# A router product with its operands exchanged, in four column groups of the TensorE array, and its accumulation over the tokens in two halves

## The chip, the cores and the metric

The kernel runs on one core of a Trainium2 chip. The metric is the device time of one execution in microseconds (us). Before the change it was 2703.0 us, the median of three runs: 2703.13, 2699.41 and 2703.0.

A core has five engines, each with its own instruction queue. TensorE (PE in the profile; PEld is its loading of stationary operands, the "weights") multiplies matrices into PSUM. VectorE (DVE), ScalarE (ACT) and GpSimd (POOL) work on tiles of 128 partitions in SBUF and PSUM. SyncE (SP) issues most DMA transfers. A semaphore orders the engines wherever one needs what another has made.

## What is computed

The weight of a first layer is corrected by a low-rank product, quantized to a codebook of 32 levels, and corrected again. Its output goes through a second layer and, beside it, through a mixture of eight small experts of rank 16; the input is added at the end. Cut to what matters:

```python
lora_delta = lora_B @ lora_A * (LORA_ALPHA / LORA_RANK)          # 32 / 64
cb = codebook / jnp.clip(jnp.max(jnp.abs(codebook)), 1e-08)
wg = (weight + lora_delta).reshape(O, I // GROUP, GROUP)         # groups of 128
normalized = wg / jnp.exp(scale_log)
idx = jnp.searchsorted((cb[:-1] + cb[1:]) * 0.5, normalized, side='left')
w_eff = (cb[idx] * scale).reshape(O, I) + lora_delta             # in value
x1 = x @ w_eff.T                                                 # first layer

result = x1 @ W_base.T + b_base
ax = x1 @ A_w.T                                                  # rank 16
probs = softmax(x1 @ router_w.T)                                 # 8 experts
per_expert = einsum('bsr,erq->bseq', ax, cores)
mixed = einsum('bseq,bse->bsq', per_expert, probs)
result = result + mixed @ B_w.T * SCALING                        # 32 / 16
return x + result
```

There are 4096 tokens of 2048 features, and both layers have 2048 outputs; all is float32. `A_w` and `router_w` stand one below the other as 24 rows (16 of rank, 8 of experts); the kernel gets them transposed, as `raT`.

## The kernel before

No value of the first layer is computed for a token. The kernel makes the product of both layers' weights, Wc = W_base · w_eff + identity (the identity carries the added input), and the product of the 24 rows with w_eff, and multiplies the tokens by these.

**Stage a** makes the weights, in 16 strips of 128 input features (`NS` = 16; `strip[i]` gives their order). A strip `a` is a tile of 128 partitions by 16 chunks of 128 (`NM` = 16). The order of the instructions is written out by hand: `quantize(i, at)` (L537) goes through the 28 levels from 3 to 30 of strip i, and after each level issues what `behind(r, f, ...)` (L719) has hung behind round r = level - 3. So the rounds of strip i carry the making ready of strip i+1 and the products of strip i-1. Every engine executes its queue in the order in which this program issues.

- `raise_to` (L527) is a round: ScalarE writes a mask into one of two buffers of `mpool` (L532), and VectorE puts the level's value where the mask is set (L533).
- For strip i+1 ScalarE also scales the low-rank correction (L496, rounds 7 and 11) and makes the lowest levels (`level_0`: L509, L512, L514, at rounds 10, 12, 14 and, for the second half, 16, 18, 20); GpSimd does `normalize`, `more_levels` and, at a strip's end, `straight_through` (L552 to L554; on VectorE for the last strip).
- `products(i-1, bs, c)` (L703) multiplies a quarter (4 chunks) of the strip by two of the four output blocks b of W_base: blocks 2 and 0 behind rounds 2, 5, 8 and 11, blocks 3 and 1 behind 17, 20, 22, the last quarter at the start of the next strip. `wb` (blocks 0 and 1) stays in SBUF, `wbp` (2 and 3) is streamed by SP in pieces (L485). A correction `low_rank` (L589) ends each pair.
- `multiply_router(i-1)` (L609), behind round 13, is the product with the 24 rows: 16 matmuls with a chunk of `a` as weights (128 columns) and 24 streamed columns (L612), plus a low-rank one (L615). `keep_router` (L623, round 22) copies the 128x24 result to `rac`, whose 32 columns (`RP` = 32) were cleared by a memset (L256).
- `keep(i, b)` (L618) empties a block's PSUM tile on ScalarE (L620) and stores it in `wc_dram` (L621): blocks 2 and 0 behind rounds 17 and 19, 3 and 1 behind rounds 5 and 6 of the next strip.
- All products of a strip share `psum_m`, three PSUM tiles that are used in turn: m_2, m_0, m_r (the router), m_3, m_1. So m_3 waits until keep has emptied m_2, m_1 waits for m_0's, and the next strip's m_0 waits for m_3's.
- `load_route(i-1)` (L627, round 9) loads the strip's 128 features of all 4096 tokens in four tiles `xs`, and `route` (L634), at the start of the second strip after it, multiplies them by `rac`: eight matmuls of 512 tokens, four to each of two PSUM tiles `acc`, in four groups of 32 array columns (`tile_position`). The sums run over all 16 strips.
- GpSimd makes from `wc_dram` the sums that stage b needs, and SP stores them in `s_dram` (`outer_w`, `inner_some`, `put`, L311 to L349).

After the last strip (L796 to L818) its products follow without other rounds between them. Here ScalarE's queue issues the stores of `wc_dram`, and `late_columns` (L677) makes the last sums on VectorE, from two fetches into tiles named late and last, stored by GpSimd's queue.

**Stage b** (from L821) multiplies the tokens by Wc in the fast scheme with seven products in place of eight, applied twice: 49 products a group of tokens (`product`, L902), each of one 1 MB tile `s` (L856) and a tile of tokens or of differences of tokens (`xA`, `xB`, `xC`, loaded at L850; differences `t` at L880). Its pools take the SBUF that stage a's pools leave, so a tile of stage b can be written only when the tiles of stage a on the same addresses are done with.

The router's product and its place, as the program has it:

```python
for m in range(NM):
    nc.tensor.matmul(ps[:, :NRA], strips[i]["a"][:, m, :], ra_sb[:, m, :], start=(m == 0), stop=False)
nc.tensor.matmul(ps[:, :NRA], strips[i]["la"][:R], lora_r, start=False, stop=True)
...
behind(13, multiply_router, i - 1)
behind(17, keep, i - 1, 2)
```

The first operand after the output is the stationary one (the weights), the second is streamed.

Of the kernel before, what the change touches and what calls it, by code (L numbers as in the profile page):

```python
# [20 lines left out]
P = 128  # L21
# [161 lines left out]
def adaln_ffn_kernel(  # L183
# [72 lines left out]
    nc.gpsimd.memset(rac, 0.0)  # L256
    cb = const.tile([P, K], F32, name="cb")
    ident = const.tile([P, P], F32, name="ident")
    ones = const.tile([P, 1], F32, name="ones")

# [7 lines left out]
    def constants():  # L268
# [3 lines left out]
        nc.gpsimd.tensor_copy(ones, ident[:, Q : Q + 1])  # L272
        for j in range(1, 4):
            nc.gpsimd.tensor_tensor(ones, ones, ident[:, RP * j + Q : RP * j + Q + 1], ALU.add)
# [87 lines left out]
    with ExitStack() as sa:  # L362
# [4 lines left out]
        xsp = sa.enter_context(tc.tile_pool(name="xsp", bufs=4))  # L367
# [106 lines left out]
        ra_sb = cl.tile([P, NM, NRA], F32, name="ra_sb")  # L474
        nc.sync.dma_start(ra_sb, raT)
# [82 lines left out]
        lora_r = cl.tile([R, NRA], F32, name="lora_r")  # L558
# [19 lines left out]
        def lora_router():  # L578
            ps = psum_m.tile([P, OQ], F32, tag="m", name="lc_r")
            for m in range(NM):  # L580
                nc.tensor.matmul(
                    ps[:R, :NRA], lora_B_sb[:, m, :], ra_sb[:, m, :], start=(m == 0), stop=(m == NM - 1)
                )
            nc.scalar.mul(lora_r, ps[:R, :NRA], LORA_SCALE)
# [24 lines left out]
        def multiply_router(i):  # L609
            ps = psum_m.tile([P, OQ], F32, tag="m", name=f"m_{i}_r")  # L610
            for m in range(NM):
                nc.tensor.matmul(  # L612
                    ps[:, :NRA], strips[i]["a"][:, m, :], ra_sb[:, m, :], start=(m == 0), stop=False
                )
            nc.tensor.matmul(ps[:, :NRA], strips[i]["la"][:R], lora_r, start=False, stop=True)  # L615
            strips[i]["r"] = ps

# [5 lines left out]
        def keep_router(i):  # L623
            nc.scalar.copy(rac[:, strip[i], 0:NRA], strips[i]["r"][:, :NRA])


        def load_route(i):  # L627
            strips[i]["x"] = []
            for n in range(4):
                x = xsp.tile([P, 2 * HT], F32, tag="xs", name=f"xs_{i}_{n}")  # L630
                nc.sync.dma_start(x, xT[ts(strip[i], P), ts(n, 2 * HT)])
                strips[i]["x"].append(x)

        def route(i):  # L634
            for n in range(8):
                j = n % 4
                nc.tensor.matmul(
                    acc[n // 4][RP * j : RP * j + RP],
                    rac[:, strip[i], :],
                    strips[i]["x"][n // 2][:, ts(n % 2, HT)],  # L640
# [587 lines left out]
```

## Time and profile before

| what | value |
|---|---|
| median of three runs | 2703.0 us (2699.41 to 2703.13) |
| the profiled execution | 2701.32 us |
| its span | 2699.5 us |
| mean granted TensorE clock | 0.971 of full speed |
| PE busy | 2562.5 us (95%) |
| DVE busy | 1574.9 us (58%) |
| ACT busy | 1117.8 us (41%) |
| POOL busy | 1300.1 us (48%) |
| HBM traffic over the span | 215 GB/s |

The span is what lies between the first and the last instruction in the trace; the execution's own time has a little around it. The shares are means over two unlike stages, as the page's slices show: each digit is the busy share of one of 40 equal slices (67.5 us each), in tenths.

```profile
PE   4699999999999999999799999999999999999999
DVE  9999999999999999973423213233123322224321
ACT  6888988999998888840000000000000000000000
```

The first 17 or 18 slices are stage a, where VectorE and TensorE are both full and ScalarE nearly so; the rest is stage b, TensorE's products alone. The chain that ended last, by engine and by line:

```profile
PE 59%; DVE 22%; ACT 8%; DMA 5%; issue 3%; SPq 2%; POOL 1%; DVEq 0%; POOLq 0%; ACTq 0%
PE z L902 49%; DVE a L533 21%; PE m L601 8%; ACT above L532 6%; PE z L932 1%; DMA wbp<-in_wbT 1%; DMA s<-s_dram 1%; DMA xA<-in_xT 1%; ACT out L620 1%; DMA s_dram<-late_z 1%; ACT a L514 1%; SPq L347 1%; SPq L348 0%; DMA s_dram<-z 0%; ACT sg L509 0%
```

How to read a group: line, engine, operation, output and inputs with their shapes, count | busy us, mean ns of one | idle time of the engine just before them, with what ended most of it. A float32 matmul of the program is two matmul records in the trace (two passes). A row of the timeline has start, length (us), engine, line, what it does, count, and in brackets the idle time before it and its releaser.

### The profile page before, as it was taken

The numbers are of one execution on the slowest core, as the hardware profiler recorded it, in microseconds if no ns is written. First come the engines' busy times: TensorE is split into PE (matmuls) and PEld (weight loads), VectorE is DVE, ScalarE is ACT, GpSimd is POOL, SyncE is SP. The second block draws the span as 40 slices with busy tenths as digits, with TensorE's granted clock in tenths as the row PEclk, the third lists the DMA queues.
The fourth block names the chain that finished last, engine by engine and source line by source line (L and its number), as shares of the span: only waits on it lengthen the run. The fifth ranks groups of instructions, "written<-read, shape, count | busy, mean of one in ns | idle before, by whom it ended". The sixth has DMA issues, their size and how long they took to land.

```text
span 2699.5 us, 26233 instructions
## 1 busy us (share of the span) xinstructions
PE 2562.5 (95%) x10544; PEld 1761.5 (65%) x10544; DVE 1574.9 (58%) x995; ACT 1117.8 (41%) x740; POOL 1300.1 (48%) x751
## 2 busy tenths in 40 slices
PE   4699999999999999999799999999999999999999
PEld 2244444444444444445688888888888888888887
DVE  9999999999999999973423213233123322224321
ACT  6888988999998888840000000000000000000000
POOL 5666668889888888744304232033310313302324
PEclk9799999999999999999899999999999999999999
DMA  7345457766776767699744666545675455854554
GB/s 283 138 167 178 178 174 246 233 229 225 244 242 232 244 219 237 209 314 324 300 174 143 231 245 217 208 142 209 213 264 186 171 206 181 292 194 171 186 198 163
DMA packets 222809, 581.06 MB, mean 215 GB/s; under 512 B 18328, under 2 KB 120608, under 8 KB 177760
## 3 DMA queue, kind: packets, MB, share of 16 engines
q1 hardware_dynamic: 216448, 559.01, 60.2%
q0 software_dynamic: 4640, 13.90, 1.4%
q10 hardware_dynamic: 1600, 6.49, 0.6%
q8 instruction: 83, 1.36, 0.2%
q14 instruction: 38, 0.31, 0.0%
HBM read 477.62 MB, written 101.71 MB: 215 GB/s over the span
## 4 chain that ended last, share of the span: by engine, by line
PE 59%; DVE 22%; ACT 8%; DMA 5%; issue 3%; SPq 2%; POOL 1%; DVEq 0%; POOLq 0%; ACTq 0%
PE z L902 49%; DVE a L533 21%; PE m L601 8%; ACT above L532 6%; PE z L932 1%; DMA wbp<-in_wbT 1%; DMA s<-s_dram 1%; DMA xA<-in_xT 1%; ACT out L620 1%; DMA s_dram<-late_z 1%; ACT a L514 1%; SPq L347 1%; SPq L348 0%; DMA s_dram<-z 0%; ACT sg L509 0%
## 5 line engine op out<-in xcount | busy, mean ns | idle before, releaser
L533 DVE COPY_PREDICATED a<-above,step 128x2048 f32<-128x2048 uint16 (+1 forms) x453 | 1116.5, 2468 | 51.1 <-ACT above L532 5.7
L532 ACT ACTIVATE above<-w,neg_t 128x2048 bf16<-128x2048 f32 (+1 forms) x453 | 899.4, 1991 | 141.7 <-DVE a L533 128.8
L902 PE MATMUL z<-t,s 128*128 128x256 f32 x3584 | 793.5, 381 | 7.1 <-DMA s<-s_dram 7.1
L902 PEld LDWEIGHTS z<-t,s 128*128 128x128 f32 x3584 | 679.1, 190 | 110.9 <-issue 20.0
L601 PE MATMUL m<-wbp,a 128*128 128x512 f32 x1024 | 506.7, 641 | 43.0 <-POOL a L554 35.7
L601 PE MATMUL m<-wb,a 128*128 128x512 f32 x1024 | 467.0, 599 | 26.6 <-ACT out L620 26.6
L601 PEld LDWEIGHTS m<-wbp,a 128*128 128x128 f32 x1024 | 205.7, 206 | 294.4 <-issue 243.9
L601 PEld LDWEIGHTS m<-wb,a 128*128 128x128 f32 x1024 | 194.7, 192 | 276.6 <-issue 238.7
L982 ACT COPY m<-z 128x1024 f32<-128x1024 f32 x28 | 28.4, 1013 | 766.0 <-PE z L902 766.0
L902 PE MATMUL z<-xA,s 128*128 128x256 f32 x1152 | 256.2, 381 | 12.4 <-DMA s<-s_dram 12.4
L993 POOL TENSOR_TENSOR c<-u,m 128x1024 f32<-128x1024 f32 x16 | 50.1, 3129 | 444.1 <-DVE u L990 422.8
L902 PEld LDWEIGHTS z<-xA,s 128*128 128x128 f32 x1152 | 219.8, 191 | 43.7 <-issue 13.6
L521 POOL TENSOR_SCALAR lv<-w,base 128x1024 f32<-128x1024 f32 x60 | 226.9, 3782 | 3.7
L993 POOL TENSOR_TENSOR M<-u,m 128x1024 f32<-128x1024 f32 x8 | 25.7, 3208 | 354.1 <-DVE u L990 296.4
L902 PE MATMUL z<-xB,s 128*128 128x256 f32 x768 | 169.7, 379 | 0.0
L902 PE MATMUL z<-xC,s 128*128 128x256 f32 x768 | 169.7, 379 | 0.0
L984 DVE TENSOR_TENSOR u<-z,m 128x1024 f32<-128x1024 f32 x28 | 34.3, 1223 | 219.0 <-issue 175.5
L902 PEld LDWEIGHTS z<-xB,s 128*128 128x128 f32 x768 | 145.9, 190 | 19.8
L902 PEld LDWEIGHTS z<-xC,s 128*128 128x128 f32 x768 | 145.9, 190 | 19.8
L988 ACT COPY m<-z 128x1024 f32<-128x1024 f32 x28 | 28.3, 1011 | 308.5 <-PE z L902 308.5
L522 POOL TENSOR_TENSOR a<-a,lv 128x1024 f32<-128x1024 f32 x60 | 142.5, 2375 | 18.4 <-ACT a L514 13.8
L552 POOL TENSOR_TENSOR a<-a,w 128x1024 f32<-128x1024 f32 x30 | 71.3, 2376 | 144.3 <-DVE a L533 144.3
(206 smaller groups left out, 1916.6 us busy)
## 6 DMA issues: line engine op xcount, KB each, us to landing
s<-s_dram SPq DMA_DIRECT2D x196, 1024.0 KB, 4.9
wbp<-in_wbT SPq DMA_DIRECT2D x131, 1024.0 KB, 5.2
xs<-in_xT SPq DMA_DIRECT2D x64, 512.0 KB, 7.2
xA<-in_xT SPq DMA_DIRECT2D x24, 1024.0 KB, 9.9
s_dram<-z SPq DMA_DIRECT2D x84, 256.0 KB, 5.6
xB<-in_xT SPq DMA_DIRECT2D x16, 1024.0 KB, 10.6
outT<-M SPq DMA_DIRECT2D x16, 1024.0 KB, 12.7
w<-in_weight SPq DMA_DIRECT2D x15, 1024.0 KB, 7.3
```

The costliest lines, as they stand in the source:

```text
L347: q.dma_start(to[:, n, 1:3, g, c], y[:, n, 1])
L521: v.tensor_scalar(lv, half(i, f, "w"), base[:, c + 1 : c + 2], base[:, c : c + 1], ALU.is_gt, ALU.mult)
L522: v.tensor_tensor(a, a, lv, ALU.add)
L532: nc.scalar.activation(above[:, c], q, AF.Relu, bias=neg_t[:, r : r + 1])
L533: nc.vector.copy_predicated(a, above[:, c].bitcast(U16), step[:, r : r + 1].to_broadcast([P, F // n]))
L552: v.tensor_tensor(a, a, w, ALU.subtract)
L601: nc.tensor.matmul(ps, strips[i]["a"][:, CM * c + m, :], t[:, m, :], start=c == 0 and m == 0, stop=False)
L902: nc.tensor.matmul(z[:, c, :], s[:, k, ts(c, P)], rhs[:, k, :], start=not more and k == 0 and c % PER == 0, stop=k == NK - 1 and c % PER = ...
L982: nc.scalar.copy(temp("m1", o), z["a"])
L984: nc.vector.tensor_tensor(temp("u2", o), z["b"], state["m1", o], ALU.add)
L988: nc.scalar.copy(temp("m5", o), z["c"])
L993: lambda d: nc.gpsimd.tensor_tensor(d, state["u3", o], state["m5", o], ALU.add),
```

## The change

- `ra_sb` has 32 columns in place of 24, the last eight cleared by a memset on VectorE, so its load goes into pieces of 24 of 32 columns. `lora_r` has 32 columns too.
- `multiply_router` exchanges the operands: a chunk of `ra_sb` (32 columns) is stationary and a chunk of the strip (128 columns) streams. Chunk m goes to the group m mod 4 of 32 array columns, and so to 32 partitions of the PSUM tile of its own; the low-rank matmul adds to the first group. The result is 24 of 32 rows by 128 features, in four partial sums.
- `router_parts` (new), behind round 16 and so between the second L509 and the next mask on ScalarE, copies the four partial sums (128x128) to SBUF, as `raw`.
- `router_sum` (new), behind round 17 after the first quarter of blocks 3 and 1, multiplies `raw` as weights by `stack`, four 32x32 unit matrices one below the other, which turns the result back and adds the four parts. `stack` is made in `constants()` by GpSimd.
- `keep_router` copies all 32 columns of `rac`, so its memset goes.
- `load_route` and `route` work on a half of the tokens at a time: `xs` has two buffers in place of four. The first half is loaded behind round 9 as before and multiplied at the start of the second strip after it; the second half is loaded there and multiplied behind round 8, between the second and third quarter of blocks 2 and 0. After the last strip its second half takes the mask buffers of `mpool`.
- After the last strip the parts follow in the order that the diff shows.

```diff
--- before.py
+++ after.py
@@ -253,11 +253,12 @@
     dram = ctx.enter_context(tc.tile_pool(name="dram", bufs=1, space=DRAM))
 
     rac = const.tile([P, NS, RP], F32, name="rac")
-    nc.gpsimd.memset(rac, 0.0)
     cb = const.tile([P, K], F32, name="cb")
     ident = const.tile([P, P], F32, name="ident")
     ones = const.tile([P, 1], F32, name="ones")
 
+    stack = const.tile([P, RP], F32, name="stack")
+
 
     accs = [const.tile([P, HT], F32, name=f"accs_{h}") for h in range(2)]
 
@@ -270,7 +271,9 @@
         nc.gpsimd.memset(cores_sb, 0.0)
 
         nc.gpsimd.tensor_copy(ones, ident[:, Q : Q + 1])
+        nc.gpsimd.tensor_copy(stack, ident[:, 0:RP])
         for j in range(1, 4):
+            nc.gpsimd.tensor_tensor(stack, stack, ident[:, RP * j : RP * j + RP], ALU.add)
             nc.gpsimd.tensor_tensor(ones, ones, ident[:, RP * j + Q : RP * j + Q + 1], ALU.add)
         for j in range(4):
             nc.sync.dma_start(cores_sb[:, j, 0:Q], cores)
@@ -364,7 +367,7 @@
 
         lap = sa.enter_context(tc.tile_pool(name="lap", bufs=4))
         cl = sa.enter_context(tc.tile_pool(name="cl", bufs=1))
-        xsp = sa.enter_context(tc.tile_pool(name="xsp", bufs=4))
+        xsp = sa.enter_context(tc.tile_pool(name="xsp", bufs=2))
         spool = sa.enter_context(tc.tile_pool(name="spool", bufs=2))
         wcp = sa.enter_context(tc.tile_pool(name="wcp", bufs=3))
         big1 = sa.enter_context(tc.tile_pool(name="big1", bufs=1))
@@ -471,8 +474,10 @@
                 m = ts(h, NM // 2)
                 nc.sync.dma_start(t[:, m, :], wbT[b][:, m, :])
             wb.append(t)
-        ra_sb = cl.tile([P, NM, NRA], F32, name="ra_sb")
-        nc.sync.dma_start(ra_sb, raT)
+        ra_sb = cl.tile([P, NM, RP], F32, name="ra_sb")
+        nc.vector.memset(ra_sb, 0.0)
+        nc.sync.dma_start(ra_sb[:, :, 0:NRA], raT)
+        raw = cl.tile([P, P], F32, name="raw")
         NC = 4
         CM = NM // NC
         stream = [(b, c) for b in range(NST, NB) for c in range(NC)] * (NS + 1)
@@ -555,7 +560,7 @@
 
 
         lora_c = cl.tile([2 * R, NB // 2, OQ], F32, name="lora_c")
-        lora_r = cl.tile([R, NRA], F32, name="lora_r")
+        lora_r = cl.tile([R, RP], F32, name="lora_r")
 
         def lora_columns(pair):
             ps = psum_m.tile([P, OQ], F32, tag="m", name=f"lc_{pair}")
@@ -579,9 +584,9 @@
             ps = psum_m.tile([P, OQ], F32, tag="m", name="lc_r")
             for m in range(NM):
                 nc.tensor.matmul(
-                    ps[:R, :NRA], lora_B_sb[:, m, :], ra_sb[:, m, :], start=(m == 0), stop=(m == NM - 1)
+                    ps[:R, :RP], lora_B_sb[:, m, :], ra_sb[:, m, :], start=(m == 0), stop=(m == NM - 1)
                 )
-            nc.scalar.mul(lora_r, ps[:R, :NRA], LORA_SCALE)
+            nc.scalar.mul(lora_r, ps[:R, :RP], LORA_SCALE)
 
         def low_rank(i, bs):
             for b in bs:
@@ -607,13 +612,27 @@
                 load_piece(nc.scalar if i == NS - 1 else nc.sync)
 
         def multiply_router(i):
+
             ps = psum_m.tile([P, OQ], F32, tag="m", name=f"m_{i}_r")
             for m in range(NM):
+                j = m % 4
                 nc.tensor.matmul(
-                    ps[:, :NRA], strips[i]["a"][:, m, :], ra_sb[:, m, :], start=(m == 0), stop=False
+                    ps[RP * j : RP * j + RP, 0:P], ra_sb[:, m, :], strips[i]["a"][:, m, :],
+                    start=m < 4, stop=m >= NM - 4 and j > 0, tile_position=(0, RP * j),
+                    skip_group_check=True,
                 )
-            nc.tensor.matmul(ps[:, :NRA], strips[i]["la"][:R], lora_r, start=False, stop=True)
+            nc.tensor.matmul(
+                ps[0:RP, 0:P], lora_r, strips[i]["la"][:R], start=False, stop=True,
+                tile_position=(0, 0), skip_group_check=True,
+            )
             strips[i]["r"] = ps
+
+        def router_parts(i):
+            nc.scalar.copy(raw, strips[i]["r"][:, 0:P])
+
+        def router_sum(i):
+
+            nc.tensor.matmul(strips[i]["r"][:, P : P + RP], raw, stack, start=True, stop=True)
 
         def keep(i, b):
             out = spool.tile([P, 4, BC], F32, tag="out", name=f"out_{i}_{b}")
@@ -621,23 +640,25 @@
             (nc.scalar if i == NS - 1 else nc.sync).dma_start(wc_dram[i // 4][b][:, i % 4], out)
 
         def keep_router(i):
-            nc.scalar.copy(rac[:, strip[i], 0:NRA], strips[i]["r"][:, :NRA])
-
-
-        def load_route(i):
-            strips[i]["x"] = []
-            for n in range(4):
-                x = xsp.tile([P, 2 * HT], F32, tag="xs", name=f"xs_{i}_{n}")
-                nc.sync.dma_start(x, xT[ts(strip[i], P), ts(n, 2 * HT)])
-                strips[i]["x"].append(x)
-
-        def route(i):
-            for n in range(8):
-                j = n % 4
+            nc.scalar.copy(rac[:, strip[i], :], strips[i]["r"][:, P : P + RP])
+
+
+        def load_route(i, h):
+            for n in range(2):
+                if i == NS - 1 and h == 1:
+                    x = mpool.tile([P, F], BF16, tag="above", name=f"xs_{i}_{h}{n}").bitcast(F32)
+                else:
+                    x = xsp.tile([P, 2 * HT], F32, tag="xs", name=f"xs_{i}_{h}{n}")
+                nc.sync.dma_start(x, xT[ts(strip[i], P), ts(2 * h + n, 2 * HT)])
+                strips[i]["x", 2 * h + n] = x
+
+        def route(i, h):
+
+            for j in range(4):
                 nc.tensor.matmul(
-                    acc[n // 4][RP * j : RP * j + RP],
+                    acc[h][RP * j : RP * j + RP],
                     rac[:, strip[i], :],
-                    strips[i]["x"][n // 2][:, ts(n % 2, HT)],
+                    strips[i]["x", 2 * h + j // 2][:, ts(j % 2, HT)],
                     start=i == 0,
                     stop=i == NS - 1,
                     tile_position=(0, RP * j),
@@ -722,7 +743,8 @@
             if i > 1:
 
                 products(i - 2, (3, 1), NC - 1)
-                route(i - 2)
+                route(i - 2, 0)
+                behind(0, load_route, i - 2, 1)
                 behind(5, keep, i - 2, 3)
                 behind(6, keep, i - 2, 1)
             if i + 1 < NS:
@@ -741,11 +763,13 @@
             if i > 0:
 
 
-                behind(9, load_route, i - 1)
+                behind(9, load_route, i - 1, 0)
                 for c in range(2):
                     behind(2 + 3 * c, products, i - 1, (2, 0), c)
                 if i + 1 < NS:
                     behind(7, delta, i + 1, 1)
+                if i > 1:
+                    behind(8, route, i - 2, 1)
                 for c in range(2, NC):
                     behind(2 + 3 * c, products, i - 1, (2, 0), c)
                 behind(13, multiply_router, i - 1)
@@ -753,7 +777,9 @@
                 behind(19, keep, i - 1, 0)
                 for c in range(NC - 1):
                     behind((17, 20, 22)[c], products, i - 1, (3, 1), c)
+                behind(17, router_sum, i - 1)
                 behind(22, keep_router, i - 1)
+                behind(16, router_parts, i - 1)
                 if i + 2 < NS:
                     behind(20, load_la, i + 2)
             else:
@@ -795,10 +821,10 @@
 
         last = NS - 1
         products(last - 1, (3, 1), NC - 1)
-        route(last - 1)
+        route(last - 1, 0)
+        load_route(last - 1, 1)
         keep(last - 1, 3)
         keep(last - 1, 1)
-        load_route(last)
         for h in range(2):
             first_fetch(h)
             first_make(h)
@@ -806,14 +832,21 @@
         for bs in ((2, 0), (3, 1)):
             for c in range(NC):
                 products(last, bs, c)
+                if bs[0] == 2 and c == 1:
+                    route(last - 1, 1)
+                    for h in range(2):
+                        load_route(last, h)
             if bs[0] == 2:
                 multiply_router(last)
+                router_parts(last)
             for b in bs:
                 keep(last, b)
             if bs[0] == 2:
+                router_sum(last)
                 keep_router(last)
                 late_columns()
-        route(last)
+        for h in range(2):
+            route(last, h)
         for h in range(2):
             nc.scalar.copy(accs[h], acc[h])
```

## The prediction, made before the changed kernel ran

> **What bounds the kernel now.** I read the page's chain of waits and its groups first, then one steady strip's windows and timelines, then the stretch after the last strip. The largest pair of groups:
>
> ```profile
> L533 DVE COPY_PREDICATED a<-above,step 128x2048 f32<-128x2048 uint16 (+1 forms) x453 | 1116.5, 2468 | 51.1 <-ACT above L532 5.7
> L532 ACT ACTIVATE above<-w,neg_t 128x2048 bf16<-128x2048 f32 (+1 forms) x453 | 899.4, 1991 | 141.7 <-DVE a L533 128.8
> ```
>
> VectorE's predicated copies run almost without a gap: 28 a strip at 2.57 us from start to start make 72.0 of a strip's 72.4 us. ScalarE's masks mostly wait for them. The window from one strip's first products on (columns: PE, PEld, DVE, ACT, POOL busy with counts, granted clock, DMA share, GB/s):
>
> ```profile
> 1054.00:1126.00 72.00, 68.52 (x206) 31.58 (x205) 69.15 (x28) 64.69 (x41) 61.18 (x39) 0.95 0.71 235
> ```
>
> TensorE is nearly as full as VectorE, but not the limit: in each strip it stands idle about 4.5 us, waiting for GpSimd's strip (L554) and twice for ScalarE to empty a PSUM tile (L620). Two of these waits, and the router between them, in a strip where the clock was whole, and the same router in the strip before, where the chunk ahead ran at half clock (5.40 instead of 3.70 us):
>
> ```profile
> 983.85 5.40 PE L601 MATMUL m<-wb,a 128*128 128x512 f32 x8 [2.06 <-ACT out L620]
> ...
> 1012.13 4.42 PE L612 MATMUL m_r<-ra_sb,a 128*128 128x24 f32 x32
> ...
> 1056.38 3.70 PE L601 MATMUL m<-wb,a 128*128 128x512 f32 x8 [1.38 <-ACT out L620]
> ...
> 1082.95 3.75 PE L612 MATMUL m_r<-ra_sb,a 128*128 128x24 f32 x32
> 1086.64 0.60 PE L615 MATMUL m_r<-lora_r,la 64*128 64x24 f32 x2
> ```
>
> ScalarE in the same strip, from the second L509 on:
>
> ```profile
> 1084.41 1.13 ACT L509 ACTIVATE sg<-w,neg_t 128x1024 bf16<-128x1024 f32 x1
> 1085.45 1.99 ACT L532 ACTIVATE above<-w,neg_t 128x2048 bf16<-128x2048 f32 x1
> 1087.35 0.56 ACT L620 COPY out<-m 128x512 f32<-128x512 f32 x1
> ...
> 1096.06 3.94 ACT L532 ACTIVATE above<-w,neg_t 128x2048 bf16<-128x2048 f32 x2
> 1099.91 0.16 ACT L624 COPY rac<-m_r 128x24 f32<-128x24 f32 x1
> 1100.60 2.00 ACT L532 ACTIVATE above<-w,neg_t 128x2048 bf16<-128x2048 f32 x1 [0.54 <-DVE a L533]
> ```
>
> No idle time stands at any row of these 15 us: here ScalarE, not VectorE, sets the pace, and its two mask buffers are used up by the end. VectorE waits for ScalarE in nearly every strip at this place (18 waits, 4.8 us together). What is added to ScalarE between L509 and the last of these masks reaches VectorE whole, and VectorE sets the end of the strip.
>
> **The router on TensorE.** It has 16 matmuls of two passes, 3.75 us, that is 117 ns a pass, though only 24 columns stream: the 128-column weight load sets it. After the change the weights have 32 columns and 128 stream, four column groups side by side. The nearest row with this shape of weights:
>
> ```profile
> L637 PE MATMUL acc<-xs,rac 128*32 128x512 f32 x224 | 26.9, 598 | 0.0
> L637 PEld LDWEIGHTS acc<-xs,rac 128*32 128x32 f32 x224 | 5.8, 109 | 19.0 <-issue 15.2 <-ACT above L532 3.8
> L624 ACT COPY rac<-m_r 128x24 f32<-128x24 f32 x14 | 2.2, 159 | 0.0
> L620 ACT COPY out<-m 128x512 f32<-128x512 f32 x56 | 31.7, 565 | 0.0
> ```
>
> In its timeline four passes start together and their four weight loads take 0.13 us, 33 ns each. So 32 passes make 1.06 us, plus 0.40 for L615's two: 1.46. Bounds: 27 ns a pass (109/4) gives 1.26; 62 ns (L581, 64-column weights, 32 passes in 2.0 us) gives 2.4; with no overlap, 117 ns as now, 4.15. I take 1.46, since L637 has the same column groups. TensorE thus saves 2.7 us a strip, less some 0.25 for the new sum (two passes of the 0.38 us pair at L605, at most 0.4). This gives no time: it has 4.5 us of idle already, and what comes next, m_3, waits for keep's copy on ScalarE. It will only wait longer.
>
> The skill speaks for the swap: "TensorEngine Tiling (Array Packing)", section "Performance Considerations", advises exchanging stationary and streaming operand with four column tiles at a free dimension of 32; by a factor of four the 3.75 us would be 0.94. The same section warns that after such a speed-up the copy out of PSUM may become the bottleneck, and the rows above show just that engine without idle time.
>
> **The new copy on ScalarE.** raw (128x128 out of PSUM) goes in directly after the second L509, ahead of the next mask. Between 159 ns for 24 columns and 565 for 512 lies 0.83 ns a column: 245 ns. Rows in that stretch start some 0.1 us before the one ahead ends, so it takes about 0.2 us of the queue (0.06 by L624's row so shortened, 0.46 by L620's). In 14 strips: +2.8 us (0.8 to 6.4). rac's copy grows from 24 to 32 columns, 7 ns: nothing, behind the mask that VectorE's 0.54 us covers.
>
> **The copy's wait for the router.** raw also waits for TensorE, and behind it on ScalarE stand the mask, keep(2), and all that VectorE runs on. From the start of the router to the end of L509 there are now 2.6 us in this strip (1082.95 to 1085.54), 2.04 to 2.82 in eleven strips, but only 0.75 to 1.05 in the three where the chunk before ran at half clock. The change also puts half of route(i-2), eight passes and 0.97 us (half of 1.92), into TensorE's queue ahead of the router, behind the last wait for ScalarE, so it is not absorbed: taken from the strip's start, where L554 sets the time, it gains nothing there. The lead is then 1.5 us in usual strips, against 1.46: a wait of 0 to 0.1, 11 strips by 0.1 makes +1 (0; by 62 ns a pass 1.0 each, +11). In half-clock strips the lead is about 0 and the wait 1.5 to 1.6. The half clock comes on a grid that drifts against the strips; it meets the 3.4 us after the 2 us idle time in three of 14 now. TensorE idles some 3 us longer in each strip, so I take four: +6.4 (three 4.8; six 9.6).
>
> The clock as the rows show it: after each router come 3.41 or 6.83 us in which the granted clock is half. "TensorE: Matmul & The Clock Gate", Part 1, says that a free-running window of 3413 ns decides, which fits these lengths; by its rule an idle window sends the clock down, so the longer idle time would make half-clock strips commoner.
>
> **Start.** ra_sb gets a memset on VectorE ahead of the first L533; by 525 ns for L256's 128x512 on GpSimd, 0.15 to 0.55: +0.3. Its DMA waits for that, at about 19.5 instead of 14.5 us, with the first three wbp loads queued behind it on SP; TensorE first needs them near 51 us and idles 26.6 us around 81 to 108, which covers it. constants() adds four small GpSimd operations (191 ns each by L274) in 20 us of idle; L256's memset goes.
>
> **The route loads.** xs_i keeps two buffers instead of four; in a strip the second half is issued at round 0 behind route(i-2,0), used after 14 us, and the load takes 7.2: hidden. Uncovered, TensorE would wait ahead of the router and the wait above would grow by as much.
>
> **After the last strip.** TensorE runs without a gap from 1159.6 to 1258.4. The router saves 2.7 there, but m_3 waits for raw and keep(2) on ScalarE and the sum costs a stall of about 0.5; stage a ends at about 1257. The chain shows what follows:
>
> ```profile
> 1196.92 10.32 DMA wbp<-in_wbT
> 1207.31 20.98 DMA xA<-in_xT
> 1228.37 6.53 DMA wc_dram<-out
> ...
> 1280.66 26.83 DMA s<-s_dram
> ```
>
> xA was loaded at 1207; in the changed layout its space is shared with the strip's xs and masks, so on SP it must wait for route(15), at 1257, and s_0 to s_2 and the last eight fetches queue behind it. Its products then begin at about 1266 instead of 1258.4. Against that the second wc_dram store no longer waits for xA (1225.5, not 1228.4), so the late columns are 3 to 4 us earlier, and TensorE stood idle 12.4 and 7.1 us for s anyway. The DMA engines, 0.99 busy from 1200 to 1265 and 0.62 from 1270 to 1280, must move the same bytes. I take -2: bounds -12.6 (all of the idle 12.4) and +10 (xA's 2 MB and s_0 to s_2 behind the end of stage a).
>
> **Sum.** 0.3 + 2.8 + 1 + 6.4 - 2 = +8.5 us on the profiled execution's 2701.3 (span 2699.5 and 1.8 around it, 1.7 under the median of 2703.0): 2710. About 0.2%, 5.4 us, is what a measurement of this kernel can tell from no change.
>
> **Rivals.**
> - Only the copies cost: the router is early in every strip, since the chunk before runs at full clock, and the tail gives back 2. 0.3 + 2.8 - 2 = +1: 2702 to 2706, the same. For it: the lead of 1.5 is as long as the router. Against: three strips have no lead. Chance 0.22.
> - The other side, faster: freed from xA at 1207, the late columns and with them s_3 and s_4 come earlier, and TensorE's idle 12.4 and 7.1 us shrink. With 3 to 4 us of masks' cost, it decides from 9 us on in the tail: 2690 to 2697. For it: the chain runs through xA's 20.98 us. Against: the bytes remain, and xA's own wait. Chance 0.2.
> - The column groups do not overlap: router 4.15, wait 2.7 in 14 strips: +38, 2740; at 62 ns a pass +11 +10 (four strips of 2.5) + 2.8 = 2723. For it: 128 streamed columns in place of 24. Against: L637's bursts. Chance 0.1.
> - The tail pays: xA and s behind 1257 push s_3 and s_4 by 10: 2722. Chance 0.08.
> - TensorE's 2.5 us in 16 strips shows in full: 2663. The 4.5 us of idle speak against it; under 0.01.
>
> My forecast has 0.4, with its own range of 2706 to 2716. Slower: 0.4, 0.1 and 0.08, of the forecast's share 0.03 falls within 0.2%: 0.55. Same: 0.25. Faster: 0.2. The range, 2694 to 2732, leaves out about a tenth at either end.
>
> **What would show it.** Right: L533's idle time rises by 5 to 12 us, released by L532; a new ScalarE group of 14 to 16 copies of about 245 ns with idle time <-PE in three to six strips; L612 near 1 us; m_3's wait for L620 near 3 us; xA issued after 1257. Wrong: raw never waits; strips keep 72.4 us; or TensorE's idle time before L902 changes by over 5 us.

## The result, and the profile after

The changed kernel takes 2717.4 us (median of four runs, 2715.78 to 2719.56) against 2702.9 us (the kernel before with a fourth run): 1.0057 times the kernel before, with a 95% interval of 1.0040 to 1.0075. It is 14.5 us slower, where 2710 had been forecast; the profiled execution took 2716.19 us, with a span of 2714.4.

The two traces were laid side by side at two points that every version has: the end of VectorE's last predicated copy (the end of the strips), and the end of TensorE's last wait for a tile s, from which on its products run without a gap to the end.

| | strips end at | from there until TensorE is fed | the rest of the span | span |
|---|---|---|---|---|
| before | 1188.3 | 119.3 | 1391.9 | 2699.5 |
| after | 1193.4 | 129.1 | 1391.9 | 2714.4 |
| difference | +5.1 | +9.8 | 0 | +14.9 |

The rows behind the second point, first before, then after:

```profile
1291.82 8.67 PE L902 MATMUL z<-xA,s 128*128 128x256 f32 x32 [12.42 <-DMA s<-s_dram]
1307.62 9.29 PE L902 MATMUL z<-t,s 128*128 128x256 f32 x32 [7.13 <-DMA s<-s_dram]
```

```profile
1285.12 9.08 PE L935 MATMUL z<-xA,s 128*128 128x256 f32 x32 [17.94 <-DMA s<-s_dram]
1322.51 9.14 PE L935 MATMUL z<-t,s 128*128 128x256 f32 x32 [7.59 <-DMA s<-s_dram]
```

So in these two executions a third of the loss lies in the strips, two thirds in the 120 us behind them, and stage b itself is untouched.

**The strips.** The groups of the page that answer to those of before (the mask is now L537, the predicated copy L538):

```profile
L538 DVE COPY_PREDICATED a<-above,step 128x2048 f32<-128x2048 uint16 (+1 forms) x453 | 1117.2, 2470 | 55.0 <-ACT above L537 14.2
L537 ACT ACTIVATE above<-w,neg_t 128x2048 bf16<-128x2048 f32 (+1 forms) x453 | 899.2, 1992 | 140.5 <-DVE a L538 127.7
```

The work is the same to 0.1%; VectorE's idle time that the masks end has grown from 5.7 to 14.2 us. The new groups, by form, up to 1195 us:

```profile
L619 PE MATMUL m_r<-a,ra_sb 128*32 128x128 f32 x480 | 16.2, 276 | 0.0
L635 PE MATMUL m_r<-stack,raw 128*128 128x32 f32 x30 | 4.6, 235 | 0.0
L631 ACT COPY raw<-m_r 128x128 f32<-128x128 f32 x15 | 3.8, 251 | 3.4 <-PE m_r L624 3.1
```

The column groups do overlap: 15 routers take 16.2 us, 1.08 us each, where one took 3.75. The copy takes 251 ns. Its 3.1 us of waiting lie in two strips. One of them, in the timelines of TensorE, ScalarE and VectorE:

```profile
551.32 5.40 PE L606 MATMUL m<-wb,a 128*128 128x512 f32 x8 [2.08 <-ACT out L639]
...
580.59 1.08 PE L619 MATMUL m_r<-a,ra_sb 128*32 128x128 f32 x32
581.60 0.40 PE L624 MATMUL m_r<-la,lora_r 64*32 64x128 f32 x2
584.73 5.40 PE L606 MATMUL m<-wbp,a 128*128 128x512 f32 x8 [2.73 <-ACT out L639]
```

```profile
579.37 1.13 ACT L514 ACTIVATE sg<-w,neg_t 128x1024 bf16<-128x1024 f32 x1
582.04 0.27 ACT L631 COPY raw<-m_r 128x128 f32<-128x128 f32 x1 [1.54 <-PE m_r L624]
582.20 2.00 ACT L537 ACTIVATE above<-w,neg_t 128x2048 bf16<-128x2048 f32 x1
```

```profile
584.24 5.05 DVE L538 COPY_PREDICATED a<-above,step 128x2048 f32<-128x2048 uint16 x2 [1.64 <-ACT above L537]
```

A chunk at half clock (5.40 us; the granted clock was 0.51 from 551.7 to 555.1) makes the router late, ScalarE stands 1.54 us at the copy, the mask behind it is late, and VectorE stands 1.64 us. The router saves 2.7 us, and m_3 behind it waits 2.73 us for ScalarE, where the trace of the kernel before marks 0.93 us at most, and 1.53 in the last strip: TensorE's gain is idle time.

**After the strips.** TensorE and SyncE's queue in the changed kernel:

```profile
1212.11 1.05 PE L658 MATMUL acc<-xs,rac 128*32 128x512 f32 x4 [1.22 <-DMA xs<-in_xT]
1215.57 1.92 PE L658 MATMUL acc<-xs,rac 128*32 128x512 f32 x4 [2.40 <-DMA xs<-in_xT]
1217.42 5.34 PE L606 MATMUL m<-wbp,a 128*128 128x512 f32 x8
...
1265.25 1.92 PE L658 MATMUL acc<-xs,rac 128*32 128x512 f32 x16
```

```profile
1199.10 0.36 SPq L351 DMA_DIRECT2D s_dram<-z  x1
...
1200.43 0.34 SPq L490 DMA_DIRECT2D wbp<-in_wbT  x1
1200.88 0.85 SPq L652 DMA_DIRECT2D xs<-in_xT  x2
...
1267.23 1.68 SPq L883 DMA_DIRECT2D xA<-in_xT  x2
1269.09 3.93 SPq L889 DMA_DIRECT2D s<-s_dram  x3
1273.07 17.41 SPq L309 DMA_DIRECT2D last<-wc_dram  x8
```

Two things are new. The second half of strip 14's route waits 1.2 and 2.4 us for its xs, which SyncE could issue only at 1200.9, behind GpSimd's last put; the next chunk then takes 5.34 in place of 3.6 us, at a granted clock of 0.68. And xA, which the kernel before loaded at 1207, is issued at 1267, when the last route is done, with s and the last fetches behind it. The window from 1240 to 1255 shows what that leaves unused (DMA share and GB/s stand last); first before, then after:

```profile
1240.00:1255.00 15.00, 15.00 (x37) 6.61 (x35) 10.27 (x27) 0.00 (x0) 8.98 (x13) 1.00 0.98 371
```

```profile
1240.00:1255.00 15.00, 15.00 (x38) 6.73 (x37) 6.69 (x18) 0.00 (x0) 3.19 (x5) 1.00 0.63 199
```

### The profile page after: what moved, and what is told of

It is laid out like the page before. It is cut to its first block, busy times and chain, and to the rows that moved or that the text cites. A ratio compares the mean times of both kernels' runs of the same rounds, so it can differ in the third digit from the quotient of the medians.

```text
span 2714.4 us, 26333 instructions
## 1 busy us (share of the span) xinstructions
PE 2517.1 (93%) x10576; PEld 1708.8 (63%) x10576; DVE 1576.5 (58%) x996; ACT 1120.2 (41%) x756; POOL 1299.7 (48%) x754
## 4 chain that ended last, share of the span: by engine, by line
PE 60%; DVE 23%; ACT 11%; DMA 3%; issue 3%; POOL 1%; DVEq 0%; SPq 0%; POOLq 0%
PE z L935 50%; DVE a L538 23%; ACT above L537 7%; PE m L606 7%; DMA s<-s_dram 1%; PE z L965 1%; ACT sg L514 1%; ACT sg L517 1%; ACT out L639 1%; DMA w<-in_weight 1%; ACT a L519 1%; DMA xs<-in_xT 1%; ACT a L501 0%; PE acc L658 0%; PE mx_ps L1102 0%
## 5 line engine op out<-in xcount | busy, mean ns | idle before, releaser
L538 DVE COPY_PREDICATED a<-above,step 128x2048 f32<-128x2048 uint16 (+1 forms) x453 | 1117.2, 2470 | 55.0 <-ACT above L537 14.2
L537 ACT ACTIVATE above<-w,neg_t 128x2048 bf16<-128x2048 f32 (+1 forms) x453 | 899.2, 1992 | 140.5 <-DVE a L538 127.7
```

Source lines behind the costliest of these rows:

```text
L537: nc.scalar.activation(above[:, c], q, AF.Relu, bias=neg_t[:, r : r + 1])
L538: nc.vector.copy_predicated(a, above[:, c].bitcast(U16), step[:, r : r + 1].to_broadcast([P, F // n]))
```

## The experiments

Each starts from the changed kernel. Ratios are to the kernel before, with 95% intervals; the stretches are those of the table above, each from one profiled execution, and the stretch behind the second point is 1391.4 to 1392.8 us in all of them. The kernel before was measured again with each group of runs (2701.6 to 2702.8 us), so medians of different groups compare to about 1 us.

| run | median us | ratio | strips end at | until fed |
|---|---|---|---|---|
| after | 2717.4 | 1.0057 (1.0040 to 1.0075) | 1193.4 | 129.1 |
| e1: three xs buffers | 2713.2 | 1.0035 (1.0022 to 1.0048) | 1196.7 | 123.2 |
| e2: tail's half route behind the router | 2719.5 | 1.0062 (1.0046 to 1.0079) | 1196.5 | 129.6 |
| e3: late copy, rac at round 25 | 2748.3 | 1.0172 (1.0157 to 1.0188) | 1225.1 | 128.2 |
| e4: the old router | 2710.6 | 1.0032 (1.0020 to 1.0044) | 1189.0 | 129.2 |
| e5: late copy, rac at round 27 | 2708.8 | 1.0027 (1.0016 to 1.0037) | 1187.2 | 127.2 |
| e6: e1 and e2 | 2709.2 | 1.0032 (1.0020 to 1.0044) | 1192.8 | 121.4 |
| e7: e1, e2 and e5 | 2700.9 | 0.9996 (0.9987 to 1.0005) | 1187.8 | 120.4 |
| e8: e7, ra_sb cleared by GpSimd | 2703.5 | 1.0004 (0.9995 to 1.0012) | 1188.4 | 118.3 |
| e9: e7, strip 15's xs behind the late fetches | 2700.6 | 0.9995 (0.9987 to 1.0004) | 1186.5 | 120.6 |
| e10: half route behind the router in the strips | 2707.0 | 1.0023 (1.0014 to 1.0032) | 1191.4 | 121.6 |
| e11: e9 with the old router | 2701.8 | 0.9999 (0.9990 to 1.0008) | 1186.5 | 118.5 |
| e12: e2, strip 15's xs behind the late fetches | 2713.3 | 1.0045 (1.0028 to 1.0061) | 1192.4 | 122.1 |

Single executions differ: in e1, e2, e6 and e12, which issue the same instructions in the strips as the changed kernel, these end at 1192.4 to 1196.7. Even so the two kinds do not overlap: with the copy at round 16 the strips end at 1191.4 or later in all six traces, without it (e3 apart) at 1189.0 or earlier, the kernel before among them. In time, every execution of each experiment but e2 and e3 lies below every one of the changed kernel, for e12 by 0.6 us only.

**e1: is it xA's wait?**

```diff
-        xsp = sa.enter_context(tc.tile_pool(name="xsp", bufs=2))
+        xsp = sa.enter_context(tc.tile_pool(name="xsp", bufs=3))
```

> Three xs buffers in place of two; nothing else differs from the changed kernel, and 4 KB more per partition shift the layout so that the first xA tile no longer shares its space with the last strip's xs. Theory (after the last strip the changed kernel pays for xA's wait for the last route): xA is issued near 1215 us instead of 1267, and TensorE's idle time before its first products falls from 17.9 + 7.6 to about the 12.4 + 7.1 of the kernel before, so 2717.4 becomes about 2711. Rival (the transfers after stage a carry the same bytes, the wait is only their sum): xA goes out early, but the idle time moves to a later product and the time stays within 2 us of 2717.

SyncE and TensorE:

```profile
1211.11 4.78 SPq L883 DMA_DIRECT2D xA<-in_xT  x2
```

```profile
1303.36 9.67 PE L935 MATMUL z<-xA,s 128*128 128x256 f32 x32 [14.89 <-DMA s<-s_dram]
1319.81 9.97 PE L935 MATMUL z<-t,s 128*128 128x256 f32 x32 [6.79 <-DMA s<-s_dram]
```

The stretch behind the strips is 5.9 us shorter, as expected, and the median falls by 4.2. The strips of this execution were 3.3 us longer: the copy waited for the router in four of them instead of two. TensorE's idle time fell to 21.7 us only (25.5 after, 19.5 before), so xA is not the whole of it. Nor are the 5.9 us xA's alone: the third buffer also lets one load of xs start without waiting for a route, and TensorE's wait for xs fell from 3.6 to 1.6 us.

**e2 and e12: is it TensorE's wait for xs?** After the last strip:

```diff
-                if bs[0] == 2 and c == 1:
-                    route(last - 1, 1)
-                    for h in range(2):
-                        load_route(last, h)
             if bs[0] == 2:
                 multiply_router(last)
+                route(last - 1, 1)
+                for h in range(2):
+                    load_route(last, h)
...
                 late_columns()
```

In e12 the two lines of load_route stand behind late_columns().

> After the last strip alone, the second half of strip 14's route moves from the middle of blocks 2 and 0 to behind the router; the loads of strip 15's xs move with it. Theory (TensorE stood there 1.2 + 2.4 us for xs, which was issued only at 1200.9, and ran its next chunk at half clock, 5.34 in place of 3.6): none of the three remains, stage a ends 5 to 6 us earlier, and 2717.4 becomes about 2712. Rival (the end of stage a is not what the first products wait for): TensorE's idle time before them grows by what was won and the time stays within 2 us of 2717.

> As the run that moved the second half of strip 14's route behind the router (two xs buffers, xA late), but the loads of strip 15's xs go behind the late columns' fetches on SP. It tells why that run gained nothing: there the late columns' first VectorE instruction came at 1249.4, behind 2 MB of xs loads that the edit itself had put ahead of their fetches. Theory (TensorE's wait for xs costs the stretch after the last mask, and in that run its gain was given back by the xs loads): from the end of the last mask to the end of TensorE's last wait for s it takes 121 to 124 us instead of 129, and 2717.4 becomes 2709 to 2713. Rival (xA's wait for the last route alone sets the stretch): 128 us or more, 2716 or more.

In e2 the three losses in TensorE's queue are gone and stage a ends 4.9 us earlier, in an execution whose strips were 3.1 us longer; the stretch is as long as before the edit (129.6 us), and TensorE's waits for s grew by 5.0 us (25.5 to 30.5). So the rival's account came out, with 2719.5 us. SyncE and the late columns on VectorE, in e2:

```profile
1231.31 3.26 SPq L652 DMA_DIRECT2D xs<-in_xT  x4
1234.62 11.42 SPq L309 DMA_DIRECT2D late<-wc_dram  x8
```

```profile
1249.37 2.62 DVE L319 TENSOR_TENSOR late<-late 128x512 f32<-128x512 f32 x4 [43.90 <-DMA late<-wc_dram]
```

and in e12:

```profile
1224.45 12.06 SPq L309 DMA_DIRECT2D late<-wc_dram  x8
1236.55 3.96 SPq L652 DMA_DIRECT2D xs<-in_xT  x4
```

```profile
1240.30 2.62 DVE L319 TENSOR_TENSOR late<-late 128x512 f32<-128x512 f32 x4 [38.81 <-DMA late<-wc_dram]
```

The edit of e2 had itself put 2 MB of xs directly ahead of the late fetches. With the two changed round, the late columns come 9.1 us earlier (4.1 of it because the strips of this execution were shorter) and the stretch is 122.1 us, 7.5 less than in e2 and 7.0 less than in the changed kernel, though xA still waits:

```profile
1258.90 1.63 SPq L882 DMA_DIRECT2D xA<-in_xT  x2
```

The rival of e12 falls in this trace: xA's wait is not alone. In time the run gave 4.1 us, just past the theory's upper end (four executions, 2707.69 to 2715.22). The profile is of the fastest of them, 5.6 us below the median, so the stretch of the others may be longer.

**e6: the two together.** Both edits above (three buffers, and e2's).

> Three xs buffers and, after the last strip, the second half of strip 14's route behind the router: the two edits together. Theory (the two hide each other: with xA at 1267 the end of stage a is not what the first products wait for, with xA early it is, since keep and the late columns follow it): with xA early, the earlier keep(2) brings the late columns forward by about 4 us and the time falls to about 2709, 4 below three buffers alone. Rival (with xA early the transfers alone set the first products): within 1.5 us of three buffers alone, 2712 to 2714.

121.4 us and 2709.2, the theory's number. e2's edit, which alone left the stretch as it was, takes 1.8 us more off it once xA is early (123.2 to 121.4). The gains of e1 (5.9) and e12 (7.0) do not add, though: with both edits, and e5's, e9 below stands at 120.6, 8.5 less than the changed kernel. That both fill the same unused transfer time is the likely reason; it was not measured by itself.

**e4: is it the transposed product at all?**

```diff
-                    ps[RP * j : RP * j + RP, 0:P], ra_sb[:, m, :], strips[i]["a"][:, m, :],
...
+                    ps[:, P : P + RP], strips[i]["a"][:, m, :], ra_sb[:, m, :], start=(m == 0), stop=False
...
-                behind(17, router_sum, i - 1)
-                behind(16, router_parts, i - 1)
```

> The router goes back to the untransposed product (with 32 columns), without the copy of the parts and the sum; the halves of the route, two xs buffers and the layout stay as in the changed kernel. Theory: the strips lose the 4.9 us that they cost, as with the late copy, and after the last strip the router is 2.3 us longer and the chunk behind it runs at half clock again, so about 2717.4 - 4.9 + 3 = 2715 to 2716: most of the 14.5 us belong to the two halves of the route and the layout, not to the transposed product. Rival (the transposed product is what costs): 2705 or less.

2710.6, between the two: the 3 us that the longer router was to cost behind the strips did not come. The strips end at 1189.0, 0.7 us behind the kernel before (0.5 of it is the memset at the start), and the stretch behind them stays at 129.2. So the strips' loss is the transposed product's, with its copy and its sum, and the long stretch belongs to the halves of the route and the layout that goes with them. By the medians the transposed product costs 6.8 of the 14.5 us.

**e3 and e5: the copy out of the full stretch.**

```diff
-                behind(17, router_sum, i - 1)
-                behind(22, keep_router, i - 1)
-                behind(16, router_parts, i - 1)
+                behind(23, router_parts, i - 1)
+                behind(24, router_sum, i - 1)
+                behind(25, keep_router, i - 1)
```

In e5 keep_router stands behind round 27.

> In the 16 strips the copy of the four parts moves from round 16 to 23, the sum to 24 and keep_router to 25, past the stretch in which ScalarE has no idle time; after the last strip nothing differs. Theory (copy and its wait pass straight to VectorE): no wait of the copy for the router remains, VectorE's waits for ScalarE fall from 13.3 us to about 5, m_3 of strip 14 starts near 1160.5 instead of 1165.0, and 2717.4 becomes about 2712.5. Rival (the strips are longer for another reason, such as TensorE's or GpSimd's waits): the strips' sum stays within 1.5 us of the changed kernel's.

> As the run with the late copy, but with keep_router behind round 27 instead of 25. There ScalarE had waited 3.0 us in each strip at keep_router, since the sum stands on TensorE behind a quarter of blocks 3 and 1 that ends near round 24, and VectorE lost 2.0 us of it. Theory (what a strip costs is whatever wait stands on ScalarE ahead of its masks; the copy at round 16 costs it by its own 0.15 us and by the router's wait at half clock): neither wait is left, a strip takes 72.4 to 72.5 us as in the kernel before, and 2717.4 becomes 2712 to 2713. Rival (a late sum holds the router's PSUM tile and so delays the next strip's m_2): strips of 73 us or more.

e3 went 31 us the wrong way, and not for its rival's reason. ScalarE and VectorE:

```profile
1069.00 0.18 ACT L643 COPY rac<-m_r 128x32 f32<-128x32 f32 x1 [3.01 <-PE m_r L635]
```

```profile
1071.12 33.27 DVE L538 COPY_PREDICATED a<-above,step 128x2048 f32<-128x2048 uint16 x13 [2.02 <-ACT above L537]
```

The edit moved the sum behind a quarter of products on TensorE, and keep_router stood 3 us for it, even where ScalarE has some idle time: VectorE lost 2 us a strip. It is the same mechanism as the copy's wait, shown larger: 14 such waits, 43.1 us together. With keep_router two rounds later (e5) the waits are gone, the strips end at 1187.2, 6.2 us earlier than in the changed kernel, and the time is 2708.8, 3 to 4 us below what was expected; the stretch behind gave 1.9 of them.

**e10: the half of the route ahead of the router.**

```diff
-                behind(9, load_route, i - 1, 0)
+                behind(15, load_route, i - 1, 0)
...
-                    behind(8, route, i - 2, 1)
+                    behind(14, route, i - 2, 1)
```

> In the strips alone, the second half of route(i-2) goes from round 8 to behind the router (round 14), and the next load of xs from round 9 to 15; the copy of the parts stays at round 16. Theory (the half ahead of the router took 0.97 us of its lead): the copy's waits for the router at half clock fall from 1.55 us to about 0.6 or vanish, its own 0.15 us a strip stay, the strips from 64.8 us on take 1016 to 1018 instead of 1019.5 us, and 2717.4 becomes 2714 to 2716. Rival (the lead is lost to the clock alone): the waits stay at 1.5 us.

The copy waits in three strips, those whose second chunk ran at half clock, and by 0.86, 0.57 and 0.56 us, about 1 us less each than the 1.53 to 1.85 (once 0.88) of such strips in the other runs. In the strips from the fourth on whose router came in time, 2.5 to 2.6 us lie between its start and the end of the second L514 (once 3.3), against 1.5 to 1.6 in the changed kernel (once 2.6): the 0.97 us are shown. One of the waits:

```profile
652.95 0.27 ACT L631 COPY raw<-m_r 128x128 f32<-128x128 f32 x1 [0.56 <-PE m_r L624]
```

The strips give 2.0 us, within what was expected of them. The time fell by 10.4, far more than expected: behind the strips SyncE issued xs at 1195.7 instead of 1200.9, so TensorE did not wait for it, and the stretch is 121.6 us, about e12's, with xA about as late as there (1258.0). GpSimd's last put came 4.9 us earlier, 2.0 of them from the strips. In SyncE's queue the last strip's load of xs stands behind the puts of that strip (1164.7) instead of among them (1153.05); that this brought them forward is likely and not shown.

**e7, e8, e9, e11: all cures, and what the idea is then worth.** e7 has the edits of e1, e2 and e5. e8 also clears ra_sb on GpSimd (`nc.gpsimd.memset(ra_sb, 0.0)`) and loads it behind three pieces of wbp. e9 is e7 with e12's order, and e11 is e9 with the old router of e4 and keep_router at round 22.

> Three xs buffers, the second half of strip 14's route behind the router, and the late copy with keep_router at round 27. Theory (the three costs add up): 2717.4 - 4.5 for the strips - 6 for xA - 3 for the late columns = 2703 to 2705, as long as the kernel before (about 2702). Rival (they do not add up): 2708 or more.

> The same, and ra_sb is cleared by GpSimd instead of VectorE and loaded behind the first three pieces of wbp. Theory: VectorE's first copies start 0.4 us earlier and nothing else moves: 0.5 us below the run before, which is at the limit of what can be measured. Rival: the later memset and load make the low-rank router product at the end of the first strip wait, and the first strip gets longer.

> As the run with all three edits, and the loads of strip 15's xs (2 MB, needed at the end of stage a) go behind the late columns' fetches on SP instead of ahead of them, where they waited for the moved route. Theory (the late columns' fetches set the first products): the first late column on VectorE starts 3 to 5 us earlier than the 1242.25 of that run, and 2701 becomes 2697 to 2699, faster than the kernel before. Rival (the transfers' bytes set it, in whatever order): within 1.5 us of 2701.

> As the first run of this call, with the router's product untransposed again (32 columns, no copy of the parts, no sum) and keep_router at round 22. It tells what the transposed product is worth once nothing else costs. Theory: the strips are equal; after the last one the router is 2.3 us longer, but m_3 waits for ScalarE's copies anyway and without the sum there is no stall, so 1 to 3 us more than the first run. Rival: the transfers set the end of that stretch and the two are equal within 1 us.

e7 takes 2700.9 us, 2 below the theory: the three edits together take away the whole loss, and with them the change is even with the kernel before (0.9996, interval across 1). In e9 the first late column starts 8.7 us earlier than in e7 (1.3 of it from the strips), and TensorE is fed within 0.2 us of e7's time behind the strips (first e7, then e9):

```profile
1242.25 2.62 DVE L319 TENSOR_TENSOR late<-late 128x512 f32<-128x512 f32 x4 [45.47 <-DMA late<-wc_dram]
```

```profile
1233.60 2.62 DVE L319 TENSOR_TENSOR late<-late 128x512 f32<-128x512 f32 x4 [38.12 <-DMA late<-wc_dram]
```

So, once xA is early, the order of these transfers does not set that stretch, as e9's rival said. That their bytes do is likely: from 1200 to 1265 the DMA engines are full in both (a share of 1.01 and 1.02), though from 1265 to 1275 they are at 0.74 and 0.61. e11 is equal to e9 within the spread (1.3 us apart, with intervals that overlap): the transposed router, freed of its costs, gains nothing that these runs can tell. e8 shows no gain either; it is 2.6 us above e7 (see the last section). No version beats the kernel before beyond its interval.

## Why the prediction was right, and where its sizes were not

The direction and the range held; the forecast of +8.5 us was a little over half of the +14.5 measured, and it put the loss in the wrong place. Step by step:

- **Router.** Forecast 1.46 us with L615's two passes, from L637's bursts; measured 1.41 (580.59 to 582.00). That it gives no time: shown, by m_3's longer wait and by e11.
- **The copy.** Forecast 245 ns, 0.2 us of ScalarE's queue; measured 251 ns, and 0.15 us from its start to the next mask's (2.1 us in 14 strips).
- **Its wait.** Forecast 1.5 to 1.6 us in half-clock strips, measured 1.54 and 1.58, and passed on to VectorE as described. The number of such strips was the error: four were taken, two came, so 3.1 in place of 6.4 us. That is a matter of the execution: the other traces with the copy at round 16 show two to four, and e1's, with four, has strips that end 8.4 us after those of the kernel before.
- **Start.** 0.47 us against 0.3.
- **The strips' sum.** Forecast +10.5 with the start, measured +5.1: 0.5 for the start, 3.1 for the waits, 2.1 for the copies, and 1.0 for one strip (near 856) in which ScalarE waited 0.9 us for GpSimd. That makes 6.7; some 1.6 us came back where nothing had been forecast. e5, without copy and waits in that place, ends its strips 1.1 us ahead of the kernel before.
- **The route loads: this step failed.** It said that the second half's load is hidden, from its 7.2 us against 14, and looked at the strips alone. After the last strip the same load stands behind GpSimd's last put and a piece of wbp, is issued 7.5 us behind VectorE's last predicated copy, and takes up to 14 us to land; nothing covers it. What it would cost when uncovered was named, but the place where the cover ends was not.
- **After the last strip: this step failed too.** It saw that xA moves to 1257 and took -2, since the late columns would come 3 to 4 us earlier and the transfers were full anyway. Measured +9.8, near its upper bound of +10. The DMA engines were at 0.63 while xA waited, and the late columns came 9.1 us later instead, 5.1 of it from the strips. The other 4.0 go with TensorE's wait for xs: this column starts 54.8 us behind the strips' end here and 53.6 in e5, which waits too, but 47.6 in e10, which does not. (The lower bound of -12.6 is 0.2 more than the 12.4 us that it names.) The first late column, before and after:

```profile
1239.06 2.62 DVE L316 TENSOR_TENSOR late<-late 128x512 f32<-128x512 f32 x4 [4.84 <-DMA late<-wc_dram]
```

```profile
1248.14 2.62 DVE L319 TENSOR_TENSOR late<-late 128x512 f32<-128x512 f32 x4 [45.74 <-DMA late<-wc_dram]
```

- **What was to show it.** VectorE's idle time rose by 3.9 us (5 to 12 had been named), the part ended by the masks by 8.5; m_3 waited 2.7 to 4.3 us; xA came at 1267. TensorE's waits for s grew by 6.0 us in all, which the prediction had named as a sign against itself, and rightly.

Of the two rules that were weighed, the swap of "TensorEngine Tiling (Array Packing)" in the Trainium skill (section "Performance Considerations") gave 3.5 of the factor of four here (3.75 to 1.08 us), and the section's warning of the copy out of PSUM came true in its own way: not the copy's 251 ns weighed, but what it waited for and who stood behind it. That longer idle time makes half-clock strips commoner, as the prediction took from "TensorE: Matmul & The Clock Gate" (Part 1) of the same skill, these traces show only in part. In the first two chunks of a strip the granted clock falls to half in nine of 14 strips, where it did in three before. But in seven of the nine it does so in the first chunk, and the second then waits less for ScalarE (0.35 us at 478.79, where 2.08 stand at 551.32), so the router is not late; only the two in the second chunk cost a wait. Behind the router the half clock became shorter: 3.41 us in eleven strips and 6.83 in one, where it had been 6.83 in 13 and 3.41 in two. That idle time is the cause of either was not tried by itself.

So the rival in which the tail pays was right as to its place, the main case as to its mechanism in the strips, and that the main case's time came as near as it did was luck: in the strips it forecast 5.4 us too much, behind them 11.8 too little.

## What to carry to other kernels

Where two engines are both nearly full, time saved on one that waits anyway is worth nothing, while an instruction with a wait, placed on the other where its queue has no idle time, costs the whole wait; look for a place some rounds later first, and then follow what waits for that. A step that is hidden in the steady loop must be checked again at the loop's end, in every queue it stands in: the cover there is another. A change of buffer counts moves the layout, and a tile of the next stage that comes to lie on one still in use can cost as much as the edit itself.

## What the runs showed that was not expected

VectorE itself stood 0.46 us seven times, about 165.6 us apart (some 64 predicated copies), in the kernel before and in e8, and in none of the other twelve traces. The waits of VectorE in the kernel before, from 100 to 1200 us (us in total, times, longest us):

```profile
DVE a L533 <- ACT above L532: 4.8, 18, 0.4
DVE a L533 <- DVE a L533: 3.2, 7, 0.5
```

The kernels without them have one more VectorE instruction, the memset of ra_sb. These 3.2 us may be where the strips' unforecast gain came from. e8 speaks for it: it differs from e7 in that memset and in the place of ra_sb's load, has the seven waits again, and took 2703.5 us in place of 2700.9, in the same group of runs, where 0.5 us less had been expected. That the waits make the difference is not shown (the two intervals overlap), and why they come stays open.
